# Three attentions of a gated cross-attention stack: reordering one hand-written step and choosing experts for four batches at once

## The chip, the cores and the metric

One NeuronCore of a Trainium2 chip runs the whole program. The metric is the device time of one execution in microseconds (us); a run of the kernel before is quoted as the median of three executions. The engines work side by side, each in the order of its own queue: TensorE (PE, with its weight loads shown as PEld), VectorE (DVE), ScalarE (ACT), GpSimd (POOL), and SyncE (SP), whose queue issues the DMAs. PSUM, into which TensorE writes, has eight banks here, and the kernel uses each bank as one tile.

## The reference, cut to what matters

A batch of 16 sequences of 128 tokens with 256 features passes through four layers. Each layer is a cross-attention and a feed-forward part, each gated by a tanh and added to the residual stream `x`. The change lies in the attentions of layers 0, 1 and 2 (16 heads of 16 features) and in the routing of layer 1's feed-forward part.

```python
x = x + tanh(g_xattn[0]) * xattn0(layernorm(x), ctx)          # 16 heads of 16
x = x + tanh(g_ffn[0])   * experts0(layernorm(x))             # one of 8 experts per token
x = x + tanh(g_xattn[1]) * xattn1(layernorm(x), ctx, rel, mask)
x = x + tanh(g_ffn[1])   * experts1(layernorm(x))             # two of 8 experts, plus a shared one
x = x + tanh(g_xattn[2]) * xattn2(layernorm(x), ctx)
x = x + tanh(g_ffn[2])   * softmoe2(layernorm(x))
...                                                            # layer 3: 16 heads of 64, then a key memory

# routing of layer 1
scores = softmax(xt @ gate_w.T)
_, indices = top_k(scores + gate_bias, 2)
weights = take_along_axis(scores, indices, axis=1)
```

## The kernel before, in words

`xattn16` computes one attention with 16 heads of 16 as a software pipeline over the 16 batches. A loop over a step number `t` calls a list of stages in a fixed order, and each stage works on batch `t - lag`. Inside `tc.manual_schedule` this call order is the order of the instructions on PE, ACT, DVE and POOL, so the list is the schedule. SP's DMAs are issued in their own queue.

In one step the stages do this, in the order before:

1. `bias_load` and `bias_make` (layer 1 only): load mask and relative-time tiles, then turn the mask into an addend: one POOL operation (`mf`, L1399) and three on DVE (L1401 to L1403).
2. `exps` (lag 4): 16 exponentials with accumulated sums on ACT (L525). In layers 0 and 2 they read the score banks in PSUM; in layer 1 the scores have already been moved to SBUF by DVE.
3. `add` and `join`: the gated residual additions on DVE (L236), in `join` of rows fetched from the previous expert stage.
4. `norm.stats` and `after.stats`: mean and variance on DVE, then a reciprocal root on POOL (`ve`, `rs`, L180 and L181), for this attention's norm and for the norm behind it.
5. `choose` (lag 9): the choice of experts from the router's logits, all on DVE. `logits` (lag 8): the router product on PE (`pr`, L657) and its first operations; in layer 1 these are a maximum on DVE (`red`, L944) and an exponential on ACT (`lg`, L947).
6. `norm.apply`, `after.apply` (`xn` or `k`, L212, on DVE, waiting for POOL's root; some also store `xn` by DMA), and `output_bias` (POOL, L483).
7. `turn` (lag 5): 16 transposes of the probabilities on PE into four banks (`pe`, L544), copied to SBUF (`eT`): all four on ACT in layer 1 (L549); two on DVE (L547) and two on ACT in layers 0 and 2.
8. Projections: `keys` or `queries` in turn, every second step each (`pk`/`kT`, `pq`/`qT`), and `value_rows` (`pv` on PE, `v` on DVE, L438).
9. `normalise` (lag 4): POOL multiplies the probabilities by their reciprocal sums (L538).
10. `scores` (lag 3): 8 matrix products into four banks (`sc`, L494), read by DVE at once: four maxima (`mx`, L503) in layers 0 and 2, or 16 fused additions with a minimum (L508) in layer 1.
11. `output` (`po`, L572), `norm.turn` (`pt`), `values` (`av`, L559) and `after.turn` (`pt`), with ACT copies `xqT`, `oT` (L565) and `rT` or `xnT`.

A step with a router takes 15 banks from the eight, a step without one 14. They are handed out in the order in which they come free. In the steady steps of layers 0 and 2 the fourth score bank (`sc3`) is the one that the first ACT copy `eT` of the same step leaves; the bank for `pv` is the one that the first DVE copy `eT` leaves. In layer 1 `sc1` takes the bank of `pv` once DVE has read it, `sc2` the router's bank once ACT has made `lg`, and `sc3` the one that the first `eT` leaves.

After the loop, `Routing.solve` places all tokens in expert order (DVE, with small products on PE), and the expert stage follows on PE.

Of the kernel before, what the change touches and what calls it, by code (L numbers as in the profile page):

```python
# [12 lines left out]
F32 = mybir.dt.float32  # L13
I32 = mybir.dt.int32
BF16 = mybir.dt.bfloat16
AF = mybir.ActivationFunctionType
ALU = mybir.AluOpType
AX = mybir.AxisListType

P = 128  # L20
B, S, D = 16, 128, 256
# [4 lines left out]
SENT = -1.0e30  # L26
FOUND = 1.0e30
# [6 lines left out]
def flamingo_gated(ctx: ExitStack, tc: tile.TileContext, a, out):  # L34
    nc = tc.nc
# [5 lines left out]
    small = ctx.enter_context(tc.tile_pool(name="small", bufs=6))  # L41
# [6 lines left out]
    def broadcast(ap, n):  # L48
        return ap.rearrange("(o n) -> o n", o=1).to_broadcast([P, n])
# [17 lines left out]
    def gate_f(layer):  # L67
        return gates[:, 4 + layer : 5 + layer]
# [9 lines left out]
        out=before, in_=ones, compare_op=ALU.is_gt, fill=0.0, base=0, pattern=[[1, P]], channel_multiplier=-1  # L78
    )
    def counting(n, step, name):  # L80

        i = const.tile([P, n], I32, name=f"{name}i")
        nc.gpsimd.iota(i, pattern=[[step, n]], base=0, channel_multiplier=0)
        f = const.tile([P, n], F32, name=name)
        nc.vector.tensor_copy(f, i)
        return f

    count = counting(P, 1, "count")
# [4 lines left out]
    part = const.tile([P, 1], F32, name="part")  # L93
# [19 lines left out]
    def load_slot(src, cols, name, queue=nc.sync):  # L113
        t = wp.tile([P, WSLOT], F32, tag="w", name=name)
        queue.dma_start(out=t[:, 0:cols], in_=src)
        return t
# [108 lines left out]
    def in_groups(tiles, n, make):  # L225


        def into(b):
            if b % n == 0:
                tiles[b // n] = make()  # L230
            return tiles[b // n][:, :, b % n * S : (b % n + 1) * S]

        return into
# [156 lines left out]
    def xattn16(layer, bias=None, after=None, joining=None):  # L390
# [7 lines left out]
        after, logits, choose = after  # L398
        with ExitStack() as es:
# [186 lines left out]
            if joining is not None:  # L586
# [3 lines left out]

            stages = (
                (1, bias_load),
                (2, bias_make),
                (4, exps),
                (7, add),
                (0, join if joining is not None else None),
                (0, norm.stats),
                (7, after.stats),
                (9, choose),
                (8, logits),  # L600
                (0, norm.apply),
                (7, after.apply),
                (0, output_bias),
                (5, turn),
                (3, value_rows),
                (4, normalise),
                (3, scores),
# [3 lines left out]
                (7, after.turn),  # L611
            )
            with tc.manual_schedule(engines=ENGINES):
                for t in range(-1, B + 9):
                    for lag, stage in stages:
                        if stage == value_rows:
                            if t % 2 and (t + 1) // 2 < B // G:
                                keys((t + 1) // 2)
                            if t % 2 == 0 and 0 < t // 2 <= B // G:
                                queries(t // 2 - 1)  # L620
                        if stage is not None and 0 <= t - lag < B:
                            stage(t - lag)


# [5 lines left out]
    def pick_mask(pool, vals, best, k, mask):  # L630

        top = pool.tile([P, 8], F32, tag="top", name="top")
        nc.vector.memset(top, SENT)
        nc.vector.tensor_copy(top[:, 0:k], best[:, 0:k])
        rep = pool.tile([P, 16], F32, tag="rep", name="rep")
        nc.vector.match_replace(out=rep, in_to_replace=top, in_values=vals, imm_value=FOUND)
        nc.vector.tensor_scalar(mask, rep[:, 0:8], FOUND, None, ALU.is_equal)
# [3 lines left out]
    class Routing:  # L641
# [18 lines left out]
        def choose(self, b, vals):  # L660
            best = self.pool.tile([P, 8], F32, tag="best", name="best", bufs=2)
            nc.vector.max(out=best, in_=vals)
            pick_mask(self.pool, vals, best, 1, self.masks[0][:, b, :])
            if len(self.masks) > 1:
                pick_mask(self.pool, vals, best, 2, self.all[:, b, :])
                nc.vector.tensor_tensor(self.masks[1][:, b, :], self.all[:, b, :], self.masks[0][:, b, :], ALU.subtract)
            nc.vector.tensor_tensor(self.cum[:, b + 1, :], self.cum[:, b, :], self.all[:, b, :], ALU.add)

        def solve(self):
# [254 lines left out]
    def attention_ffn1(joining):  # L924
        with tc.tile_pool(name="r1", bufs=1) as rp:
            wr = rp.tile([P, 2, 8], F32, name="wr1")
            nc.sync.dma_start(out=wr, in_=a["rw1"])
            gb = rp.tile([P, 8], F32, name="gb1")
            nc.sync.dma_start(out=gb, in_=broadcast(a["gb1"], 8))
            routing = Routing(1, rp, 2, NBLK1, wr)  # L930
            vals = [rp.tile([P, 16], F32, tag=f"lg{i}", name=f"lg{i}") for i in range(2)]
            for t in vals:
                nc.gpsimd.memset(t, SENT)
            weights = [const.tile([P, B], F32, tag=f"wt{i}", name=f"wt{i}") for i in range(2)]
            xnT = {}

            into = in_groups(xnT, 4, lambda: xtp.tile([P, 2, GT], F32, tag="xnT", name="xnT"))

            known = {}

            def logits(b):
                pr = routing.logits(b, xnT[b // 4][:, :, b % 4 * S : (b % 4 + 1) * S])
                red = small.tile([P, 1], F32, tag="red1", name="red")
                nc.vector.tensor_reduce(red, pr, AX.X, ALU.max, negate=True)  # L944
                lg = small.tile([P, 8], F32, tag="lg1", name="lg")
                tot = small.tile([P, 1], F32, tag="tot1", name="tot")
                nc.scalar.activation(lg, pr, AF.Exp, bias=red, accum_out=tot)  # L947
                known[b] = lg, tot

            def choose(b):  # L950
                lg, tot = known.pop(b)
                nc.vector.reciprocal(tot, tot)
                nc.vector.scalar_tensor_tensor(vals[b % 2][:, 0:8], lg, tot, gb, ALU.mult, ALU.add)
                nc.vector.tensor_tensor(tot, tot, gate_f(1), ALU.mult)
                routing.choose(b, vals[b % 2])
                for t, m in zip(weights, routing.masks):
                    own = small.tile([P, 8], F32, tag="own1", name="own")
                    nc.vector.scalar_tensor_tensor(own, lg, tot, m[:, b, :], ALU.mult, ALU.mult)
                    nc.vector.tensor_reduce(t[:, b : b + 1], own, AX.X, ALU.add)

            attention1((Norm(into, store=normed[1]), logits, choose), joining)
            ws = load_slot(a["we1"][8], 3072, "ws")
            routing.solve()

            def shared():
                shared_expert(ws, 512, xnT, gate_f(1))

            sorted_experts(routing, a["we1"][0:8], 512, shared)
        return results[1], 2, lambda i, b: weights[i][:, b : b + 1]
# [557 lines left out]
```

## Time and profile before

| what | value |
|---|---|
| median of 3 runs | 2210.04 us (2206.56 to 2211.8) |
| profiled execution, its own time | 2212.79 us |
| its span, first to last instruction | 2211.1 us |
| mean granted TensorE clock | 0.936 of full speed |
| busy: PE, DVE, ACT, POOL | 88%, 58%, 43%, 35% of the span |
| attention of layer 0 | about 24 to 207 us |
| attention of layer 1 | about 436 to 657 us |
| attention of layer 2 | about 990 to 1185 us |

The three attentions fill about 600 us. A step of the loop can be timed by the ACT copy `oT` (L565), of which there is one in each step with values. In layer 0 these copies start at 112.13, 122.51 and 132.89 us, so a step takes 10.38 us. In layer 1 they start at 530.02, 541.14, 552.80 and 566.07 us: steps of 11.12, 11.66 and 13.27 us. In layer 2 they start at 1045.26, 1055.99 and 1068.35 us: 10.73 and 12.36 us.

The lists of stretches, waits, and instructions in order of time are read like this: a bracket behind an instruction gives the idle time of the engine before it and the instruction whose end ended it. PEclk is the share of full speed that TensorE was granted.

### The profile page before, as it was taken

The numbers are of one execution on the slowest core, as the hardware profiler recorded it, in microseconds if no ns is written. First come the engines' busy times: TensorE is split into PE (matmuls) and PEld (weight loads), VectorE is DVE, ScalarE is ACT, GpSimd is POOL, SyncE is SP. The second block draws the span as 40 slices with busy tenths as digits, with TensorE's granted clock in tenths as the row PEclk, the third lists the DMA queues.
The fourth block names the chain that finished last, engine by engine and source line by source line (L and its number), as shares of the span: only waits on it lengthen the run. The fifth ranks groups of instructions, "written<-read, shape, count | busy, mean of one in ns | idle before, by whom it ended". The sixth has DMA issues, their size and how long they took to land.

```text
span 2211.1 us, 31775 instructions
## 1 busy us (share of the span) xinstructions
PE 1948.9 (88%) x10603; PEld 1319.0 (60%) x10603; DVE 1291.9 (58%) x3965; ACT 957.7 (43%) x3103; POOL 769.3 (35%) x921
## 2 busy tenths in 40 slices
PE   5996999888859999978887998949899999988787
PEld 4774566566645666655664444438776777765676
DVE  3776122267773222227766999859926667652775
ACT  5884222288851122228872111134424344434662
POOL 3653333255430145535543222200011222221675
PEclk9998999989879999999998999979999999999788
DMA  2002777511012288873002113543210000000000
GB/s 91 33 23 80 301 293 294 179 37 34 26 30 88 98 311 320 314 261 122 25 18 108 67 76 143 189 168 114 77 39 1 11 11 1 20 2 0 8 13 20
DMA packets 56563, 223.48 MB, mean 101 GB/s; under 512 B 11984, under 2 KB 31952, under 8 KB 44240
## 3 DMA queue, kind: packets, MB, share of 16 engines
q0 software_dynamic: 15312, 134.10, 16.6%
q1 hardware_dynamic: 41088, 87.36, 11.4%
q8 instruction: 84, 1.38, 0.3%
q14 instruction: 79, 0.65, 0.1%
HBM read 190.24 MB, written 31.20 MB: 100 GB/s over the span
## 4 chain that ended last, share of the span: by engine, by line
PE 25%; DVE 19%; POOL 4%; issue 4%; ACT 3%; DMA 1%; POOLq 0%; ACTq 0%; SPq 0%; DVEq 0%
PE pk L266 3%; PE pq L278 2%; PE po L361 2%; PE pv L289 2%; DVE tot L1135 2%; POOL rn L1300 2%; PE po L1155 2%; DVE d L1082 1%; DVE red L1079 1%; DVE tot L1086 1%; PE av L351 1%; DVE cw L1129 1%; PE sc L308 1%; PE pq L1237 1%; DVE cw L1137 1%
## 5 line engine op out<-in xcount | busy, mean ns | idle before, releaser
L803 PE MATMUL pg<-we,xT 128*128 128x512 f32 (+1 forms) x588 | 268.2, 586 | 1.0 <-ACT xT L197 1.0
L538 POOL TENSOR_TENSOR e<-e,sums 128x512 f32<-128x512 f32 x192 | 194.1, 1043 | 144.4 <-DVE sums L533 106.9
L809 DVE TENSOR_TENSOR h<-sg,pg 128x256 f32<-128x256 f32 x147 | 60.3, 411 | 248.0 <-ACT sg L808 201.8
L808 ACT ACTIVATE sg<-pg 128x256 f32<-128x256 f32 x147 | 55.3, 376 | 303.0 <-PE pg L803 295.5
L525 ACT ACTIVATE e<-sc,mx 128x128 f32<-128x128 f32 x512 | 179.7, 413 | 0.0
L803 PEld LDWEIGHTS pg<-we,xT 128*128 128x128 f32 x588 | 106.2, 192 | 89.1 <-issue 79.1
L778 POOL DMA_INDIRECT we<-in_we,rows x62 | 60.0, 967 | 264.3 <-PE pd L834 172.7
L834 PE MATMUL pd<-we,hT 128*128 128x256 f32 (+1 forms) x588 | 141.7, 383 | 1.2 <-ACT hT L823 1.2
L329 POOL TENSOR_TENSOR e<-e,rec 128x512 f32<-128x512 f32 x64 | 65.3, 1041 | 216.7 <-DVE rec L328 140.3
L834 PEld LDWEIGHTS pd<-we,hT 128*128 128x128 f32 (+1 forms) x588 | 109.6, 190 | 44.1 <-issue 25.8
L1155 PE MATMUL po<-yt,cT 128*128 128x256 f32 x512 | 128.2, 396 | 8.5 <-ACT cT L1147 8.4
L1098 PE MATMUL acc<-d,k 128*128 128x512 f32 x256 | 122.4, 620 | 9.7 <-POOL d L1088 9.5
L525 ACT ACTIVATION_READ_ACCUMULATOR e<-sc,mx 128x1 f32 x512 | 129.4, 253 | 0.0
L1088 POOL TENSOR_TENSOR d<-d,tot 128x1024 f32<-128x1024 f32 x32 | 62.8, 1961 | 168.4 <-DVE tot L1087 168.4
L494 PE MATMUL sc<-kT,qT 32*128 32x256 f32 x768 | 98.3, 432 | 25.0 <-DVE v L438 14.0
L1083 ACT ACTIVATE d<-d 128x1024 f32<-128x1024 f32 x32 | 33.8, 1057 | 195.5 <-DVE d L1082 189.2
L1072 PE MATMUL pl<-phi,xnT 128*128 128x512 f32 x256 | 116.5, 599 | 0.0
L544 PE MATMUL pe<-ident,e 128*128 128x128 f32 x768 | 104.1, 289 | 10.4 <-POOL e L538 10.2
L1155 PEld LDWEIGHTS po<-yt,cT 128*128 128x128 f32 x512 | 97.4, 200 | 21.4 <-ACT cT L1147 9.7
L180 POOL TENSOR_SCALAR ve<-mv 128x1 f32<-128x1 f32 (+1 forms) x136 | 26.1, 192 | 234.2 <-DVE mv L187 183.4
L544 PEld LDWEIGHTS pe<-ident,e 128*128 128x128 f32 x768 | 92.0, 152 | 17.2 <-POOL e L538 15.5
L236 DVE SCALAR_TENSOR_TENSOR x<-po,gates,x 128x256 f32<-128x256 f32 x96 | 45.4, 473 | 91.5 <-PE po L361 53.2
(291 smaller groups left out, 4538.4 us busy)
## 6 DMA issues: line engine op xcount, KB each, us to landing
ew<-in_ew SPq DMA_DIRECT2D x8, 2048.0 KB
spill<-lg SPq DMA_DIRECT2D x32, 512.0 KB
cw<-spill SPq DMA_DIRECT2D x8, 2048.0 KB
ctxT<-in_ctxT SPq DMA_DIRECT2D x16, 512.0 KB
got<-results SPq DMA_DIRECT2D x48, 128.0 KB
normed<-xn SPq DMA_DIRECT2D x32, 128.0 KB
aw<-in_aw SPq DMA_DIRECT2D x3, 1280.0 KB
x<-in_x SPq DMA_DIRECT2D x16, 128.0 KB
```

Source lines behind the costliest of these rows:

```text
L266: nc.tensor.matmul(pk, lhsT=wk[:, k, c * P : (c + 1) * P], rhs=ctxT[g][:, k, :], start=(k == 0), stop=(k == 1))
L329: nc.gpsimd.tensor_tensor(e, e, rec.unsqueeze(2).to_broadcast([P, 4, S]), ALU.mult)
L494: nc.tensor.matmul(banks[j][:, c * 256 : (c + 1) * 256].rearrange("p (i k) -> p i k", i=2), lhsT=qT[r, c, tok], rhs=kT[r, c, :, tok], star ...
L525: nc.scalar.activation(e[:, c, :], sc[:, c, :], AF.Exp, bias=mx[:, h : h + 1], scale=sign, accum_out=sums[b][:, h : h + 1],)
L538: nc.gpsimd.tensor_tensor(e, e, r, ALU.mult)
L544: nc.tensor.transpose(pe[:, c * P : (c + 1) * P], e[:, c, :], ident)
L803: nc.tensor.matmul(pg[:, 0 : 2 * m].rearrange("p (g i) -> p g i", g=2), lhsT=tokens[j][:, k, :], rhs=wgu[:, k, :, i0 : i0 + m], start=(k = ...
L834: nc.tensor.matmul(pd[:, 0:D], lhsT=hT[0:m, ic, :], rhs=wd[0:m, ic, :], start=(ic == 0), stop=(ic == nic - 1))
L1072: nc.tensor.matmul(pl, lhsT=xnT[b // 4][:, k, tok], rhs=phi[:, k, n], start=(k == 0), stop=(k == 1))
L1088: nc.gpsimd.tensor_tensor(dv, dv, tot.unsqueeze(2).to_broadcast([P, 32, 32]), ALU.mult)
L1098: nc.tensor.matmul(acc[hf][k][q], lhsT=keep[b][:, k * P : (k + 1) * P], rhs=d[:, q * 512 : (q + 1) * 512], start=(b == 0), stop=(b == B - 1),)
L1155: nc.tensor.matmul(pos[b][:, 0:D], lhsT=cT[:, c, :], rhs=yt[2 * q + c // 2][:, c % 2, :], start=(q == 0 and c == 0), stop=(q == 3 and c == 3),
```

## The change

First, four entries of the stage list move, for all three layers. `turn` goes from behind `output_bias` to a place right behind `choose`, so that its copies stand between the statistics and the norms. `logits` goes behind `bias_make`, and both go behind `output_bias`, ahead of `value_rows`. All other stages keep their order.

Second, in layer 1 `choose` no longer handles one batch per step. It collects four batches and does their work in three parts at three successive steps: scaled probabilities, sums with the bias, four maxima and two copies in the first; eight match-and-replace operations and two mask operations in the second; the second mask, the running counts and the weights in the third; nothing in the fourth. The loop is two steps longer, so that the last group can finish. The gate on the weights is applied once, at the end, to all of them.

Third, the counting line of `Routing.choose` becomes a method `count`, and its branch for two picks, which only layer 1 used, goes away. Layer 0 does the same work as before.

```diff
             stages = (
                 (1, bias_load),
-                (2, bias_make),
                 (4, exps),
...
                 (9, choose),
-                (8, logits),
+                (5, turn),
                 (0, norm.apply),
                 (7, after.apply),
                 (0, output_bias),
-                (5, turn),
+                (2, bias_make),
+                (8, logits),
                 (3, value_rows),
...
-                for t in range(-1, B + 9):
+                for t in range(-1, B + 11):
...
-                        if stage is not None and 0 <= t - lag < B:
+                        if stage is not None and 0 <= t - lag < B + (2 if stage == choose and layer == 1 else 0):
                             stage(t - lag)
...
             def choose(b):
-                lg, tot = known.pop(b)
-                nc.vector.reciprocal(tot, tot)
-                nc.vector.scalar_tensor_tensor(vals[b % 2][:, 0:8], lg, tot, gb, ALU.mult, ALU.add)
-                nc.vector.tensor_tensor(tot, tot, gate_f(1), ALU.mult)
-                routing.choose(b, vals[b % 2])
-                for t, m in zip(weights, routing.masks):
-                    own = small.tile([P, 8], F32, tag="own1", name="own")
-                    nc.vector.scalar_tensor_tensor(own, lg, tot, m[:, b, :], ALU.mult, ALU.mult)
-                    nc.vector.tensor_reduce(t[:, b : b + 1], own, AX.X, ALU.add)
+                part, g = (b + 1) % 4, slice(b // 4 * 4, b // 4 * 4 + 4)
+                if part == 0:
+                    nc.vector.reciprocal(tot[:, g], tot[:, g])
+                    nc.vector.tensor_tensor(lg[:, g, :], lg[:, g, :], wide(tot[:, g]), ALU.mult)
+                    nc.vector.tensor_tensor(vals[:, :, 0:8], lg[:, g, :], gb.unsqueeze(1).to_broadcast([P, 4, 8]), ALU.add)
+                    best = rp.tile([P, 4, 8], F32, tag="best4", name="best4")
+                    for i in range(4):
+                        nc.vector.max(out=best[:, i, :], in_=vals[:, i, :])
+                    for k, t in enumerate(tops):
+                        nc.vector.tensor_copy(t[:, :, 0 : k + 1], best[:, :, 0 : k + 1])
+                elif b >= 4 and part == 1:
+
+                    g = slice(g.start - 4, g.start)
+                    for t, mask in zip(tops, (routing.masks[0], routing.all)):
+                        rep = rp.tile([P, 4, 16], F32, tag="rep4", name="rep4", bufs=2)
+                        for i in range(4):
+                            nc.vector.match_replace(
+                                out=rep[:, i, :], in_to_replace=t[:, i, :], in_values=vals[:, i, :], imm_value=FOUND
+                            )
+                        nc.vector.tensor_scalar(mask[:, g, :], rep[:, :, 0:8], FOUND, None, ALU.is_equal)
+                elif b >= 4 and part == 2:
+                    g = slice(g.start - 4, g.start)
+                    first, both = routing.masks[0][:, g, :], routing.all[:, g, :]
+                    nc.vector.tensor_tensor(routing.masks[1][:, g, :], both, first, ALU.subtract)
+                    for i in range(g.start, g.stop):
+                        routing.count(i)
+                    for t, m in zip(weights, routing.masks):
+                        own = rp.tile([P, 4, 8], F32, tag="own4", name="own4")
+                        nc.vector.tensor_tensor(own, lg[:, g, :], m[:, g, :], ALU.mult)
+                        nc.vector.tensor_reduce(t[:, g], own, AX.X, ALU.add)
+                    if g.stop == B:
+                        for t in weights:
+                            nc.vector.tensor_scalar(t, t, gate_f(1), None, ALU.mult)
```

## The prediction

> **What bounds the kernel now.** I read the page first: PE is busy for 88% of the span, but the three attentions that the change touches are not alike, so I took them stretch by stretch (length, then busy time of PE, PEld, DVE, ACT and POOL with instruction counts, granted clock, DMA share, GB/s). One step of the first attention, two of the second, one of the third:
>
> ```profile
> 112.13:122.51 10.38, 9.86 (x90) 7.59 (x89) 7.86 (x24) 8.39 (x39) 6.35 (x10) 1.00 0.04 14
> ```
> ```profile
> 541.50:553.20 11.70, 9.43 (x88) 7.32 (x88) 10.00 (x68) 10.27 (x45) 6.69 (x11) 1.00 0.06 18
> 553.20:566.50 13.30, 11.01 (x88) 8.12 (x88) 10.80 (x74) 11.36 (x46) 7.59 (x12) 0.87 0.07 18
> ```
> ```profile
> 1045.26:1055.99 10.73, 8.73 (x86) 6.54 (x86) 8.58 (x18) 8.34 (x40) 6.21 (x10) 1.00 0.08 25
> ```
>
> No engine fills its step; each step is a ring through several engines. Next the waits of 440 to 660 us (total, times, longest), then the instructions around one release in order of time:
>
> ```profile
> PEld sc L494 <- DVE v L438: 17.8, 14, 2.3
> ...
> PEld pr L657 <- ACT xnT L197: 11.7, 16, 0.9
> ...
> DVE f L1401 <- POOL mf L1399: 7.7, 13, 1.2
> ```
> ```profile
> 548.51 2.04 ACT L549 COPY eT<-pe 128x512 f32<-128x512 f32 x4
> ...
> 549.25 1.14 PE L494 MATMUL sc<-kT,qT 32*128 32x256 f32 x14 [1.77 <-DVE v L438]
> ...
> 553.35 0.40 ACT L525 ACTIVATE e<-e,mx 128x128 f32<-128x128 f32 x1
> ```
>
> The second attention has two rings of equal length. **DVE's:** its last L508 ends at 541.81, `v` ends at 549.19, `sc` starts at 549.25, L508 again at 550.03, the last one ends at 553.49: 11.7 us. **ACT's:** exponentials from 541.70, `lg` at 548.25, first `eT` done at 549.10, the rest of `sc`, then `po`, `pt`, `av`, `pt`, the copy `xnT`, exponentials at 553.35: 11.65 us. In steps with `kT`, ACT's own work is the bound: 11.1 us without an idle moment (530.4 to 541.5).
>
> In the first attention only ACT's ring is closed: the copies start, `sc` waits for the first, and the tail follows:
>
> ```profile
> 118.23 1.17 ACT L549 COPY eT<-pe 128x512 f32<-128x512 f32 x2
> ...
> 118.97 0.72 PEld L494 LDWEIGHTS sc<-kT,qT 32*128 32x128 f32 x10 [0.18 <-ACT eT L549]
> ...
> 120.03 1.13 PE L572 MATMUL po<-aw,oT 128*128 128x256 f32 x4
> ```
>
> In the third, the chain of waits (start, length, what) runs through DVE and POOL:
>
> ```profile
> 1081.83 0.56 POOL rs L181
> 1082.39 0.03 issue
> 1082.41 0.81 DVE k L212
> 1083.22 0.61 DVE eT L547
> 1083.83 0.04 issue
> 1083.87 1.13 PE pv L434 x4
> 1085.00 1.23 PE sc L494 x14
> ```
>
> The reader is to see that `eT` stands idle behind a norm that waits for POOL, and that PE waits for `eT` to free a bank.
>
> **Part 1: the turn between statistics and norms (third attention).** DVE ends its statistics at 1081.08. POOL's two roots need until 1082.39, in which DVE waits 0.42 and 0.49 us. The two copies (1.28 us) now fill this time; the transposes they read were done by then. `pv` gets its bank at about 1081.1 + 0.64 = 1081.7 instead of 1083.8, and DVE's ring is 2.1 us shorter. What is late next is ACT's ring: from exponentials at 1079.24 to those at 1089.55, 10.31 us. So a step of 10.73 becomes 10.31, not 8.6. By the copies `oT`, steps at 1045.26, 1055.99, 1109.95 and 1120.68, and parts of slow ones at 1068.35 and 1132.16, are above 10.31, by 1.6 us together and some 0.5 for the parts: **2.1 us**. The norms and their DMA stores come 1.3 us later, but their PE readers stand 4 us behind; SP's queue holds nothing that waits for them. POOL's `output_bias` also moves by 1.3 us into 2.7 us of idle time. Cover gone, that would cost 1.3 us a step.
>
> In the first attention the same move does nothing on the ring: DVE waited 1.14 us for `pv` anyway.
>
> **Part 2: the router product behind the turn (first and second).** PE waits 0.46 to 0.52 us in each step for `rT` or `xnT` ahead of `pr`. That wait goes, as transposes fill it. Its sum over 16 steps is 8.2 us in the first attention and 7.4 in the second. It is mostly not a gain: PE reaches `sc` earlier and waits there for ACT. In the first attention a step stays at 10.38; only two steps of the drain, where PE leads, lose 0.5 each: **1 us**. The trace can't show the new hand-out of banks. `pr` no longer takes the first free bank and no longer leaves one for the fourth transposition tile, so each later tile draws another. Ends: `sc` a copy later, +0.2 us a step for 12 steps, +2.4; or `sc3` gets a bank free before the copies, and the ring opens to PE's 9.86, -0.5 for 14 steps, -7. I take 0, nearest to the row of now.
>
> In the second attention ACT no longer waits for `red` before its copies (0.29 us ahead of `lg` at 548.25) and makes `lg` (0.26) after them. But `lg` then frees the router's bank last, so I count `sc3` on the second copy (+0.48): exponentials 6.2, two copies 1.06, tail 3.8 (from 549.25 to 553.35 are 4.1, less 0.3 for `sc` already done), together **11.1**.
>
> **Part 3: `bias_make` behind `output_bias`.** DVE's wait for `mf` (0.75 us, POOL being in `normalise` until 542.15) goes from the head of the step. It returns smaller or equal behind the norms: `mf` now follows `output_bias`, which follows `xn`, so `f` starts about 1.3 us after `xn` ends, of which the second `xn` covers 0.4. Behind `f` on DVE are `red` and `v`, and PE waits for `v`. The mask load that follows `mf` moves along; it is used a step later.
>
> **Part 4: choice for four.** Before, a batch costs 20 DVE records from 545.16 to 548.06: 2.90 us. The three parts, by the spacing of the same rows: (1) reciprocal 0.16, two 128x32 operations 0.25 each, four maxima 0.15, two copies 0.2: 1.7; (2) eight match-and-replace with value load 0.25, two masks 0.2: 2.4; (3) mask 0.15, four dependent counts 0.17, four for the weights 0.22: 1.7. That is 5.8 for four, or 1.45 a batch. No row shows 128x32 with a broadcast; 0.17 (128x8) to 0.29 (128x128) bounds it, ±0.2 us per group.
>
> DVE from the last L508 to the end of `v`, worked as above, with the roots ready 3.4 us in: 5.8 (empty step), 6.1, 6.6 and 7.1 against 7.37: its ring goes to 10.1-11.3, mean 10.7. ACT's 11.1 is next. So steps with `qT` go from 11.65 to 11.1, four of them: **2.2 us**. Steps with `kT` stay. Later steps (603 to 635 us, 10.43, ACT's ring) lie between -0.26 and +0.3: 0.
>
> The drain: the last choice now takes 5.8 us, but spread behind three steps that no longer carry 2.90 each. Counting from 641.3 (2.4 and 1.7 in the first two, none in the third, then 1.7, 2.4 and up to the counts 0.9) the counts are ready at 656.1, as now (656.29, `pn` starts): 0.
>
> **The clock.** In the second attention the steps ending at 492.23, 505.61, 518.90, 566.07, 578.77 and 592.38 take 12.7 to 13.6 us, together 79.5 against 67.8 at the 11.3 of the others: 11.7 us lost, as `po` takes 2.08 us (562.40) instead of 1.13 (550.32). They begin behind PE gaps of 0.2 to 1.8 us at `sc`. The Trainium skill, "TensorE: Matmul & The Clock Gate", section "Why this matters for your kernels", puts the limit at idle gaps of about 3 us. By that rule no gap here, before or after, costs anything: 0. By the row they do cost. I take the row. PE's idle time in a `qT` step falls from 2.2 us (0.46 at `pr`, 1.77 at `sc`) to 11.1 - 9.43 = 1.7, but in one gap. The bounds are all 11.7 gained, or the same again lost; the first attention with 0.5 idle holds 1.00, the third with 2.0 mostly holds it. I take a third: **4 us**.
>
> The same page, section "Part 4: PE-mode transpose", says that transposes don't count as PE work for this gate. It would speak against a turn put straight behind `pt`'s transposes: 2.4 us of them in a row. The row says otherwise: the first attention has 0.44 + 1.94 us of transposes with only 1 us between and stays at 1.00. By the rule I would add 2 us to a third of 30 steps, +20; by the row 0.
>
> **Sum.** 2.1 + 1 + 2.2 + 4 = 9.3, and 0.9 for the one step of the second attention in which DVE's `red` itself waits for `pr`: 10.2 us. The profiled execution took 2212.8 (span 2211.1 and 1.7 around it), so 2202.6; the median of the runs is 2.8 below it: **2199.8 us**. The stages behind (PE in order behind the placing of tokens) take the whole shift.
>
> **Rivals.**
> - *The banks open ACT's ring.* First attention -7, third: `sc` behind the exponentials alone, 10.31 to 9.85 (ACT's own work with `kT`), 11 steps, -5; with the 10.2: 2187.8. For it: `eT` on DVE frees banks earlier. Against: the copies on ACT keep their place. 0.17.
> - *The clock falls where it held (slower).* Joined gaps at `sc`: about 1 us in the first attention, 1.5 in the third, where a wait at `pv` and one at `sc` were apart. If these drop at half the second's rate (6 of 13 steps), 10 of some 27 steps cost 2.0 more: +20, less the 10.2 and with the 4 us of the clock not gained: +13.8, 2223.8. It decides from five such steps on. For it: a gap of 1.28 us preceded the slow step at 485.34. Against: the third attention, 1.1 to 1.5, mostly holds. 0.22.
> - *Off the ring altogether.* ACT keeps all three, clock as before: -2, 2208. For it: ACT's ring is within 0.1 us of DVE's in the second attention. 0.16.
>
> **How the numbers follow.** Forecast 0.45, own range 2192 to 2206. No change can be told from a measurement within 0.2%, 4.4 us. Faster: 0.17 + nearly all of 0.45: 0.59; same: 0.19; slower: 0.22. The range takes in the opened ring and half of the clock's loss: 2185 to 2219.
>
> **What would show it.** In the third attention, no chain through `rs`, `k`, `eT`, `pv`, and steps near 10.3. In the second, DVE idle over 1 us a step, `sc` waiting for `eT` and not for `v`, `mf` still waited for, steps of 11.1. In the first, `pr` without a wait and 10.38 as before. Steps of 9.9 there show opened banks; clocks below 0.9 there show the slower rival. I am wrong if the second attention's steps stay at 11.65 or PE's clock there is no better than 0.87.

## The result, and the profile after

The change makes the kernel slower: 2228.87 us median of five runs (2219.49 to 2231.65) against 2211.8 for the kernel before (2206.56 to 2212.72), a ratio of 1.0073 with a 95% interval of 1.0047 to 1.0099. A second measurement (change_again below) gave 2225.03 against 2213.38, 1.0048 [1.0031, 1.0066]. The profiled execution is the quickest of the five, 2219.49 us (span 2217.8), so its trace shows 6.7 us of a loss of 12 to 17.

First the stretches of the profile after, one step each, with the columns of the prediction's list (length, busy time of PE, PEld, DVE, ACT, POOL with instructions, granted clock, DMA share, GB/s): a steady step of attention 0, then its three steps that have `pv` but neither `kT` nor `qT`; three steps of attention 1; one of attention 2.

```profile
112.08:122.47 10.39, 10.11 (x90) 7.72 (x90) 7.30 (x24) 8.39 (x40) 6.35 (x10) 1.00 0.05 14
143.24:156.07 12.83, 11.83 (x82) 8.18 (x82) 8.61 (x32) 7.65 (x37) 7.29 (x12) 0.73 0.04 12
166.23:179.13 12.90, 11.42 (x79) 7.91 (x79) 8.23 (x30) 7.28 (x37) 6.01 (x9) 0.74 0.03 11
179.13:192.13 13.00, 11.52 (x79) 7.79 (x79) 6.93 (x21) 7.31 (x37) 4.78 (x7) 0.76 0.17 52
534.60:545.94 11.34, 10.25 (x90) 7.89 (x89) 6.61 (x40) 11.04 (x46) 6.29 (x10) 1.00 0.11 33
545.94:558.88 12.94, 11.88 (x90) 8.85 (x90) 10.21 (x67) 10.07 (x43) 6.89 (x11) 0.87 0.06 17
608.85:622.50 13.65, 10.85 (x79) 7.65 (x79) 8.64 (x66) 9.07 (x40) 5.24 (x8) 0.75 0.04 12
1064.53:1074.85 10.32, 9.49 (x86) 7.19 (x86) 7.54 (x18) 9.43 (x41) 6.34 (x10) 1.00 0.09 27
```

The last steps of attention 0 before, in the same columns:

```profile
143.27:153.17 9.90, 8.45 (x82) 6.07 (x81) 7.76 (x24) 7.65 (x37) 5.87 (x10) 1.00 0.05 16
163.34:173.02 9.68, 8.16 (x80) 5.78 (x79) 6.58 (x21) 7.28 (x36) 4.29 (x6) 1.00 0.05 14
173.02:182.71 9.69, 8.17 (x80) 5.79 (x79) 6.67 (x21) 7.28 (x37) 4.79 (x7) 1.00 0.25 69
```

Steady steps do what was forecast: 10.39 and 10.32. But three steps of attention 0 grow from between 9.7 and 9.9 us to some 13, with the same work on PE, PE busy 3.3 us longer, and the clock down from 1.00 to about 0.75. They add 9.5 us, and attention 0 ends 8.9 us later (`pn`, the first product of the placing of tokens, starts at 214.95 instead of 206.03). The clock of attention 1 from its first `oT` to its last is 0.88, against 0.89 before, and the attention ends with two steps of 13.65 where before they took 10.43.

The waits of attention 1, 440 to 665 us, in the profile after (total, times, longest):

```profile
PEld sc L494 <- ACT eT L549: 18.7, 21, 3.2
...
PEld sc L494 <- DVE v L438: 11.7, 14, 2.7
...
DVE f L1431 <- POOL mf L1429: 10.7, 14, 1.2
```

`pr` is no longer among those that wait long; `sc` now waits for `eT` more than for `v`; DVE's wait for `mf` did not shrink, it grew from 7.7 to 10.7 us.

The chain of waits through one step of attention 2 (start, length, what):

```profile
1069.12 1.68 ACT e L525 x9
1070.80 0.04 issue
1070.84 1.60 PE sc L494 x12
1072.44 1.06 PE po L572 x4
1073.50 0.22 PE pt L196 x2
1073.72 1.05 PE av L559 x32
...
1074.85 0.31 ACT oT L565
```

POOL's roots and the norms are gone from it. What remains is ACT's ring: the exponentials, then `sc`, `po`, `pt` and `av` on PE, a copy, and exponentials again.

### The profile page after: what moved, and what is told of

It is laid out like the page before. It is cut to its first block, busy times and chain, and to the rows that moved or that the text cites. A ratio compares the mean times of both kernels' runs of the same rounds, so it can differ in the third digit from the quotient of the medians.

```text
span 2217.8 us, 31603 instructions
## 1 busy us (share of the span) xinstructions
PE 1964.9 (89%) x10603; PEld 1329.5 (60%) x10603; DVE 1259.6 (57%) x3791; ACT 957.2 (43%) x3103; POOL 770.3 (35%) x922
## 4 chain that ended last, share of the span: by engine, by line
PE 27%; DVE 15%; ACT 5%; issue 3%; POOL 3%; DMA 1%; POOLq 0%; ACTq 0%; SPq 0%; DVEq 0%
ACT e L525 3%; PE pk L266 2%; PE pq L278 2%; PE po L361 2%; PE pv L289 2%; DVE tot L1165 2%; POOL rn L1330 2%; PE po L1185 2%; PE acc L1128 2%; PE pl L1102 1%; PE av L351 1%; DVE cw L1159 1%; PE sc L308 1%; PE pq L1267 1%; DVE cw L1167 1%
## 5 line engine op out<-in xcount | busy, mean ns | idle before, releaser
L525 ACT ACTIVATE e<-sc,mx 128x128 f32<-128x128 f32 x512 | 179.7, 412 | 0.0
L494 PE MATMUL sc<-kT,qT 32*128 32x256 f32 x768 | 119.5, 443 | 36.2 <-ACT e L525 15.1
L1185 PE MATMUL po<-yt,cT 128*128 128x256 f32 x512 | 125.8, 391 | 11.4 <-ACT cT L1177 11.3
L494 PEld LDWEIGHTS sc<-kT,qT 32*128 32x128 f32 x768 | 65.4, 196 | 84.2 <-ACT e L525 33.2
L544 PE MATMUL pe<-ident,e 128*128 128x128 f32 x768 | 101.9, 287 | 10.7 <-POOL e L538 10.6
L1185 PEld LDWEIGHTS po<-yt,cT 128*128 128x128 f32 x512 | 95.5, 196 | 24.0 <-ACT cT L1177 12.8
```

What stands on the lines that cost most here:

```text
L494: nc.tensor.matmul(banks[j][:, c * 256 : (c + 1) * 256].rearrange("p (i k) -> p i k", i=2), lhsT=qT[r, c, tok], rhs=kT[r, c, :, tok], star ...
L525: nc.scalar.activation(e[:, c, :], sc[:, c, :], AF.Exp, bias=mx[:, h : h + 1], scale=sign, accum_out=sums[b][:, h : h + 1],)
L544: nc.tensor.transpose(pe[:, c * P : (c + 1) * P], e[:, c, :], ident)
L1185: nc.tensor.matmul(pos[b][:, 0:D], lhsT=cT[:, c, :], rhs=yt[2 * q + c // 2][:, c % 2, :], start=(q == 0 and c == 0), stop=(q == 3 and c == 3),
```

## Experiments

Each kernel was timed beside the kernel before on the same chip; ratios are to that. Rows with the same value in the third column were timed together; the groups ran on different chips, so a comparison between two groups is rougher than one inside a group.

| kernel | median us | before, beside it | ratio [95%] |
|---|---|---|---|
| choice_alone | 2210.58 | 2213.98 | 0.9982 [0.9971, 0.9994] |
| order_alone | 2227.04 | 2213.98 | 1.0054 [1.0034, 1.0073] |
| old_in_first | 2217.5 | 2213.98 | 1.002 [1.0009, 1.0031] |
| new_in_third | 2209.58 | 2213.98 | 0.9976 [0.9963, 0.999] |
| fill_full | 2216.4 | 2212.9 | 1.0016 [1.0004, 1.0028] |
| fill_turned | 2218.6 | 2212.9 | 1.0019 [1.0007, 1.003] |
| fill_corner | 2225.4 | 2212.9 | 1.0046 [1.0027, 1.0065] |
| router_ahead | 2206.48 | 2212.9 | 0.9973 [0.996, 0.9986] |
| change_again | 2225.03 | 2213.38 | 1.0048 [1.0031, 1.0066] |
| fill_two | 2210.74 | 2213.38 | 0.9991 [0.9977, 1.0005] |
| router_filled | 2204.77 | 2213.38 | 0.9955 [0.9938, 0.9972] |
| fill_in_wait | 2214.34 | 2214.72 | 0.9997 [0.9984, 1.001] |
| change_output_ahead | 2186.87 | 2214.72 | 0.9861 [0.9839, 0.9883] |
| output_ahead | 2172.84 | 2214.72 | 0.9799 [0.9776, 0.9823] |

### Which part costs, and in which attention

Four kernels take the change apart. choice_alone has the choice for four with the list of before; order_alone the new list with the choice of before; the other two use both lists (OLD and NEW stand for the two lists of the diff).

```diff
 # choice_alone: the change with
-            stages = NEW
+            stages = OLD
 # order_alone: the kernel before with
-            stages = OLD
+            stages = NEW
 # old_in_first: the change with
+            if layer in (0,):
+                stages = OLD
 # new_in_third: the change with
+            if layer in (0, 1):
+                stages = OLD
```

> The choice for four, with the order of before in all three attentions. Theory A (the order costs, through the granted clock; the choice gains): attentions 0 and 2 step as before (10.38 and 10.7 us, PE clock 0.98 and 0.91); in attention 1 DVE ends its step earlier and the time falls by 2 to 6 us, to 2206 to 2210. Theory B (the choice costs: 2 us of it in one step make attention 1 uneven and its end late): 5 to 8 us slower than before, 2217 to 2220.

> The new order of stages in all three attentions, with the choice per batch of before. Theory A: attention 0 loses 9 to 10 us in its steps without keys, at a PE clock of 0.7 to 0.76 there, attention 2 gains 5, attention 1 loses 3 to 10 more than with the choice for four: 2220 to 2232. Theory B: attention 1 is no slower than before, so 2211.8 + 9.4 - 5.1 = 2216.

> The change, but with the order of before in attention 0. Theory A (attention 0 carries most of the loss): oT steps there of 10.38, 9.9 and 9.7 us at a clock of 1.00 again, and 9 us less than the change: about 2219, and less if the runs of the change that were slower than its profiled one lost their time there too. If attention 1 carries the loss of the slower runs: no less than 2219, to 2222.

> The order of before in attentions 0 and 1, the new order in attention 2, and the choice for four. Theory A: 5.1 us gained in attention 2 and 2 to 6 by the choice: 2200 to 2205, faster than both kernels. Theory B: 5 gained in attention 2, 5 to 8 lost by the choice: 2212 to 2215.

The choice gains 3.4 us alone, the order loses 13.1 alone: theory A in both. By differences of medians inside this group, the order costs 2217.5 - 2209.58 = 7.9 us in attention 1 and gains 1.0 in attention 2 (new_in_third against choice_alone, which the intervals do not separate from nothing). In attention 0 it costs about 8, by two groups: change_again lies 11.7 above its before, old_in_first 3.5 above. Theory A had put most of the loss into attention 0; it is half there and half in attention 1. old_in_first came out 1.5 us under the 2219 expected, new_in_third above its 2200 to 2205.

The profiles show why single traces mislead here. With PE's order of before and no added work (before, choice_alone, old_in_first, new_in_third and router_ahead below), 4 of the 15 steps without `kT` or `qT` in attention 0 took over 11 us, though the code of this attention is the same in the first four. With the new order (the change twice, order_alone) it was 9 of 9, each above 12.7 us. In attention 1, the time from the first `oT` to the last was 175.4, 177.9, 179.7 and 175.3 us with the new order (change, change_again, order_alone, old_in_first), and 171.4, 167.1 and 168.2 us with PE's order of before and the choice for four (choice_alone, new_in_third, router_ahead). The one trace of the kernel before has 174.0, with the choice per batch.

### Is it the clock, and what counts as work for it?

Three kernels add products to the change, between `pv` and `sc`, in just those three steps of attention 0. fill_full adds 0.83 us of PE's time to each, and fill_corner 0.84 us on a sixteenth of the array. fill_turned adds only 0.49 us: in the records a transpose of this size is one pass of about 0.27 us, a product two.

```diff
 # in value_rows, behind the products of pv
+                for n in range(3 if layer == 0 and b in (12, 14, 15) else 0):
 # fill_full
+                    nc.tensor.matmul(pv[:, 256:384], lhsT=ident, rhs=ident, start=True, stop=True)
 # fill_turned
+                    nc.tensor.transpose(pv[:, 256:384], ident, ident)
 # fill_corner
+                    nc.tensor.matmul(pv[0:32, 256:384], lhsT=ident[0:32, 0:32], rhs=ident[0:32, :], start=True, stop=True)
```

> The change, and in attention 0's three steps without kT or qT (batches 12, 14, 15 of value_rows) three extra products of the whole array (128x128 into a free part of the bank pv, 0.6 us together) between pv and sc, where PE later waits 0.8 us for ACT. Added work, nothing left out. Theory A (the clock is granted by how much of the array worked in a stretch of 3.41 us; the steps fall because pv and sc stand there without the transposes): the three steps go from 12.8 to 13.0 back to 9.9 and 9.7 us, the clock in them to 1.00, the whole 9 us less than the change. Theory B (the length of the waits decides): the same. Theory D (the steps are long for another reason than the clock, such as banks): 0.6 us more in each.

> The same with three extra transposes of the same size in place of the products. By the rule that transposes do not count as PE work the three steps stay at 12.8 to 13.0 us. Theory A with transposes counted in full, and theory B: 9.9 and 9.7 us, 9 us less than the change.

> The same with three extra products of the same length that use 32 rows and 32 columns of the array, a sixteenth of it. Theory A: hardly any help, the three steps stay at 12.8 to 13.0 us. Theory B (only PE's idle time counts): 9.9 and 9.7 us, as with the others.

fill_full: the three steps take 10.38, 10.15 and 10.15 us at a clock of 1.00 (9.9 and 9.7 were expected; the added products themselves are on the path there), and the whole falls by 0.3 to 0.6% against the change. fill_corner, timed beside it: 13.07, 12.89 and 13.06 us, as without, and a median 9.0 us above fill_full's (2225.4 against 2216.4). Adding work made the kernel faster, and the same PE time on a sixteenth of the array did not, so the clock is the cause in attention 0. fill_turned: 10.38, 11.29 and 12.74 us in its profile, one step kept and two not; its median of 2218.6 lies nearer to fill_full's than to fill_corner's. Transposes do help, and the reading "they stay at 12.8 to 13.0" falls.

The clock in the trace is either whole or half, and changes on a grid of 3.413 us: the recorded stretches last 3.413, 6.827, 10.240 us and so on. The Trainium skill, "TensorE: Matmul & The Clock Gate", section "What's actually happening", says the same: a window of 3413 ns that runs freely and does not start anew with the kernel. So PE's work has to be cut along that grid. Three such stretches of the change, around the beginning of the first long step:

```profile
141.63:145.04 3.41, 3.41 (x54) 2.92 (x52) 3.24 (x14) 2.17 (x10) 2.90 (x6) 1.00 0.26 96
145.04:148.46 3.42, 2.81 (x13) 1.74 (x12) 2.54 (x8) 3.42 (x21) 1.42 (x3) 1.00 0.12 41
148.46:151.87 3.41, 3.02 (x14) 1.73 (x13) 0.77 (x2) 2.06 (x9) 1.88 (x2) 0.50 0.01 5
```

two of the kernel before,

```profile
148.51:151.92 3.41, 2.71 (x18) 1.66 (x17) 1.79 (x4) 2.04 (x9) 1.91 (x2) 1.00 0.01 2
151.92:155.33 3.41, 2.89 (x49) 2.41 (x48) 3.17 (x15) 2.53 (x12) 2.87 (x5) 1.00 0.01 2
```

two of fill_corner,

```profile
146.41:149.82 3.41, 3.35 (x18) 2.21 (x18) 2.17 (x6) 3.41 (x22) 0.99 (x2) 1.00 0.11 38
149.82:153.24 3.42, 2.77 (x13) 1.99 (x14) 1.28 (x3) 1.56 (x6) 2.40 (x3) 0.50 0.01 2
```

and two of fill_full:

```profile
144.53:147.95 3.42, 3.25 (x19) 2.58 (x18) 2.62 (x8) 3.42 (x21) 1.41 (x3) 1.00 0.13 42
147.95:151.36 3.41, 2.71 (x17) 1.68 (x17) 1.30 (x3) 2.04 (x9) 1.90 (x2) 1.00 0.01 4
```

In the kernel before PE is busy for 2.71 us of a stretch and keeps its clock. In fill_corner it is busy for 3.35 us of 3.41, idle for 0.06, and loses it in the next stretch. Idle time is not the measure. What PE did in the change, in order of time (start, length, what; 128*128 or 32*128 is the part of the array that is used, 128x8 or 32x256 the tile; a count is of passes, two for a product and one for a transpose):

```profile
143.05 0.44 PE L196 MATMUL pt<-ident,xn 128*128 128x128 f32 x2
143.32 1.91 PE L544 MATMUL pe<-ident,e 128*128 128x128 f32 x16
145.42 0.61 PE L657 MATMUL pr<-wr,rT 128*128 128x8 f32 x4 [0.18 <-ACT e L525]
146.03 1.13 PE L434 MATMUL pv<-aw,ctxT 128*128 128x256 f32 x4
147.09 0.69 PE L494 MATMUL sc<-kT,qT 32*128 32x256 f32 x2
148.21 1.01 PE L494 MATMUL sc<-kT,qT 32*128 32x256 f32 x2 [0.43 <-ACT e L525]
149.61 2.54 PE L494 MATMUL sc<-kT,qT 32*128 32x256 f32 x12 [0.39 <-ACT e L525]
152.08 2.07 PE L572 MATMUL po<-aw,oT 128*128 128x256 f32 x4
```

and the same step in the kernel before:

```profile
144.03 0.61 PE L657 MATMUL pr<-wr,rT 128*128 128x8 f32 x4 [0.52 <-ACT rT L197]
144.50 1.94 PE L544 MATMUL pe<-ident,e 128*128 128x128 f32 x16
146.28 1.03 PE L434 MATMUL pv<-aw,ctxT 128*128 128x256 f32 x4
147.40 1.53 PE L494 MATMUL sc<-kT,qT 32*128 32x256 f32 x6
149.63 1.13 PE L494 MATMUL sc<-kT,qT 32*128 32x256 f32 x10 [0.70 <-ACT e L525]
150.69 1.13 PE L572 MATMUL po<-aw,oT 128*128 128x256 f32 x4
```

The reader is to see what stands between the last full transpose and `po`, the next full product. Before, they are 4.25 us apart (146.44 to 150.69). With the new order `pr` stands between them too: in fill_full, at a clock of 1.00, they are 5.9 us apart (144.72 to 150.62). A stretch of 3.41 us can then fall between them and hold little but `pr` with its 8 columns, `pv`, a few products `sc` and two waits.

How much is little can be counted. The passes of `pv`, with 256 columns, start 0.216 us apart at full clock, so give each pass 0.216 us times its columns over 256, times its share of the array (rows and columns used, of 128 each), once, in the middle of its record, however long that is. Passes of `sc` on different strips of 32 rows can start 0.007 us apart and overlap, up to four together; by busy time they are counted too high, or, cut to a quarter, too low. The stretch from 145.04 in the change then holds 0.86 us of `pv`, 0.12 of `sc`, 0.11 of transposes and 0.03 of `pr`: 1.12. The one from 148.51 in the kernel before, which keeps the clock, holds 0.61 of `sc`, 0.86 of `po` and 0.18 of a transpose: 1.65. In fill_corner the stretch with 3.35 us of busy time comes to 1.15; in fill_full the two come to 1.78 and 1.28, and the clock holds. In fill_turned's second and third step a stretch of 1.22 and one of 0.65 lose it.

The same count was made for all eight profiles without added work (before, the change twice, the four above, router_ahead), between the first and the last `oT` of the three attentions: 926 stretches at full clock, 113 of them followed by half clock. All 109 with less than 1.24 us were followed by half clock, and none of the 806 with more than 1.32 us; of the 11 between, 4. The eight other profiles, which played no part in setting these two figures, give the same: all 92 below 1.24 and none of 815 above 1.32 are followed by half clock, of 16 between 6. A single bound of 1.28 misplaces 2 of the 926. By plain busy time the best bound misplaces 50, with `sc` counted as a full product 61, and with transposes as nothing 104, hardly fewer than saying "never" (113). So in these kernels the clock is granted by the work done on the array in a stretch, transposes in full, and narrow products by their share.

### Putting PE's order back

```diff
                 (9, choose),
+                (8, logits),
                 (5, turn),
                 (0, norm.apply),
                 (7, after.apply),
                 (0, output_bias),
                 (2, bias_make),
-                (8, logits),
                 (3, value_rows),
```

On PE this is exactly the order of before; the copies `eT` still stand ahead of the norms, `bias_make` still behind. With the product, the operations on DVE and ACT that belong to `logits` (`red` and `lg` in attention 1) go back too.

> The change, with the router product right ahead of the turn again, so that PE's order is that of before, while the copies eT stay ahead of the norms on DVE and ACT. Theory A: attention 0 back at 10.38, 9.9 and 9.7 us with the clock of before, attention 1 no worse than with the choice alone, attention 2 as in the change: 2203 to 2209 us. If the place of the copies is what costs (ACT and DVE, banks): about the time of the change, 2224 to 2230.

2206.48, inside theory A's range, and 0.7 to 1.0% under the change by the ratios. In its profile attention 2 steps at 10.31, attention 1 at 11.12 six times in a row, and one step of attention 0's end is long (12.17). So the place of the stage `logits` carries the loss, and the place of the copies on DVE and ACT none that can be seen. That it is the product on PE and not `red`, `lg` or the hand-out of banks is shown for attention 0 by the fillers; for attention 1 this edit alone doesn't separate them.

### How much of attention 1 is the clock?

```diff
 # fill_two: fill_full, and in attention 1
+                for n in range((0, 3, 0)[layer] if b not in (12, 14, 15) else (3, 6, 0)[layer]):
 # router_filled: router_ahead with
+                for n in range((3, 6, 3)[layer] if b in (12, 14, 15) else 0):
 # fill_in_wait: fill_full, and in scores, four (eight) products ahead of the third bank's first
+                extra = (8 if b in (12, 14, 15) else 4) if layer == 1 else 0
+                        for n in range(extra if (c, j) == (0, 2) else 0):
+                            nc.tensor.matmul(banks[0][:, 256:384], lhsT=ident, rhs=ident, start=True, stop=True)
```

> The change itself, once more, so that the kernels with extra products are set against it on the same chip: 0.6 to 0.8% above before. Its profile should show the three steps of 12.8 to 13.0 us in attention 0 again, and in attention 1 ten or more steps above 12 us, though not the same ones.

> The change with extra products of the whole array between pv and sc in attentions 0 and 1: three in attention 0's steps without kT or qT, three in each step of attention 1 and six in its last three. Added work, nothing left out. Theory A (the loss of attention 1 is the clock too, by the share of the array in a stretch): attention 1 steps at 11.1 to 11.5 us with a clock of 0.95 or more between its first and last oT, and the whole is at or below before, 2200 to 2212 us. Rival (attention 1 loses by its waits for v and eT, which the clock only follows): steps of 12.8 and more stay, 0.6 us are added, 2216 to 2225.

> The router product right ahead of the turn, with three extra products in the steps of batches 12, 14 and 15 in attentions 0 and 2, and six in those of attention 1. Theory A: the steps of 12 to 13.4 us there (one in attention 0, three in 1, two in 2 in the last profile) go to 9.7 to 11, 8 to 12 us less: 2194 to 2199. If the clock is not what makes them long: 2207.

> The change, with the three extra products in attention 0 as in fill_full, and in attention 1 four extra products of the whole array (0.9 us; eight in the steps of batches 12, 14, 15) inside sc, ahead of the third bank, where PE waits 0.5 to 1.1 us for eT. Added work, nothing left out. Theory A (attention 1 loses by the clock, and the stretch that decides is the one with sc and its wait): attention 1 steps at 11.1 to 11.6 us, clock 0.95 or more from its first oT to its last, 8 to 12 us less than fill_two or fill_full: 2200 to 2206. Rival (it loses by the waits): steps of 12.8 to 13.5 remain, 2211 to 2218.

change_again shows the three steps of 12.7 to 13.0 us again; in attention 1 it has eight steps above 12 us, not ten.

fill_two hits its time, 2210.74, for another reason than it gave: attention 1 still has seven steps above 12 us, and a clock of 0.90 from its first `oT` to its last. Many of the added products fell into the stretch of the projections, which was full, and left `sc` and its wait as they were: the stretch from 520.55 us holds 3.24 us of work, the next one 0.86, all of it `sc`, and behind it the clock falls. fill_in_wait puts them there: three steps are above 12 us and the others of full length take 10.6 to 11.5, the clock is 0.96 (0.88 in the change), and the time from the first `oT` to the last is 166.1 us against 175.4 in the change. So in that profile the clock accounts for the loss between these two points. Its median, however, missed: 2214, level with before and not separated from fill_two's or fill_full's ratio. The trace shows where most of the gain went: the time from the attention's first `pk` to its first `oT` is 48.8 us against 42.5 in the change, with the added products in it and a clock of 0.76 against 0.84, so that the attention up to `pn` takes 227.2 us, against 230.1 in the change and 223.9 in router_ahead. How much of attention 1's 8 us is the clock is therefore not measured by a median. It isn't all of it: at a clock of 1.00 its full steps take 11.3 to 11.5 us with the new order and 11.12 in router_ahead, and what makes this difference was not isolated.

router_filled comes to 2204.77, above its forecast of 2194 to 2199; by its interval it isn't told apart from router_ahead. In its profile the long steps at the end of attentions 0 and 1 went (9.90, 9.68, 9.69; 10.64, 11.78, 10.66), those of attention 2 stayed (12.37, 12.05).

### A version that beats both

The chain of attention 2 after has `po` between `sc` and the copies that ACT's next exponentials stand behind. `po` needs nothing of this step. It can go ahead of `sc`, where PE waits.

```diff
                 (4, normalise),
+                (6, output),
                 (3, scores),
-                (6, output),
```

> The change, with po ahead of sc on PE in all three attentions, so that PE's wait inside sc falls behind po's 1.1 us of work and the tail behind sc is shorter by as much. If the ring through ACT and the tail is what paces the steps: 10.4 and 10.3 us go to 9.9 in attentions 0 and 2, 11.1 to about 10.6 in 1, 10 to 17 us less. Theory A on the clock: less waiting in all, but sc stands further from a product of the whole array: the steps without keys stay slow. Together 2205 to 2220. If the banks that po takes earlier hold up sc: no gain, 2225 or more.

> The router product right ahead of the turn, and po ahead of sc. By the shorter tail 5 to 15 us less than the router product alone: 2192 to 2202. If the steps are paced by something else, or banks hold up sc: 2206 or more.

Together with router_ahead's order this takes 42 us off the kernel before: 2172.84, 0.9799 [0.9776, 0.9823], below the forecast of 2192. By the ratios `po` ahead of `sc` brings 1.7% of it. Steps are 9.85 us in attention 0, 9.44 in 2 and 10.74 to 10.97 in most of 1. The chain of waits in attention 2 of output_ahead:

```profile
1054.80 1.90 PE pk L419 x8
1056.70 0.96 PE pv L434 x4
1057.66 0.86 PE po L572 x4
1058.52 2.00 PE sc L494 x16
1060.53 0.37 PE pt L196 x2
1060.89 1.01 PE av L559 x32
1061.90 0.37 PE pt L196 x2
1062.28 0.90 PE pe L544 x8
```

It is PE from end to end: no wait at `sc`, no engine between. Most of the gain is the shorter ring: at a clock of 1.00 in both, steps of attention 2 take 9.44 us instead of router_ahead's 10.31. The clock of attention 2 rises as well, from 0.94 to 0.96 between first and last `oT`. The same edit on the change gives 2186.87, also below its forecast of 2205; in attention 0 four of the steps that take 9.85 us in output_ahead take 10.38 there and the fifth 12.07, so the router product behind the turn costs in this version too (14.0 us between the two medians). Why it holds 10.38 was not followed up.

## Why the prediction was wrong

The forecast was 2199.8, faster; in direction and size the slower rival ("the clock falls where it held", 2223.8) is what happened, at 2225 to 2229. The rest of the forecast's mechanics mostly stands.

- **Bound before, and Part 1 (attention 2).** Right. Seven steps in a row take 10.32 or 10.33, forecast 10.31, and the chain left POOL and DVE for ACT's ring, as named. By medians the gain is 1.0 us, which the intervals do not separate from nothing; forecast 2.1.
- **Part 2, attention 0.** The steady step (10.38) is right, and so "I take 0" for the banks. The drain is wrong: not 1 us gained but 9 lost.
- **Part 2 and 4, attention 1.** The choice: with the order of before, steps with `qT` take 11.12 us, forecast 11.1 from 11.65, and the kernel 3.4 us less, forecast 2.2. With the change's order steps at a clock of 1.00 take 11.3 to 11.5. The 0.9 us for `red` waiting for `pr` was not won: it waits 5.2 us in five places after, against 0.9 in one before; what that costs was not isolated. `mf` is waited for 3 us longer in sum, not equal or less; router_ahead has `bias_make` in the same place and steps at 11.12, so that costs nothing that shows. The drain, forecast at 0, gained 1.7 us in the profile (13.9 us before, 12.2 after, from the last `oT` to `pn`).
- **The clock, the step that failed.** "I take a third: 4 us" gained in attention 1, and "by the row 0" for attention 0. Measured: the order costs about 8 us in each, 13.1 alone in all. In attention 0 this is the clock; in attention 1, by the profiles, the clock is a large part, not the whole. The term was built on PE's idle time in a step (2.2 against 1.7 us), and idle time doesn't decide: a stretch with 0.06 us idle lost the clock, one with 0.70 kept it. What decides is the work in a stretch of 3.41 us, and that it fell in the drain of attention 0 (the two stretches above: 1.65 before, 1.12 after) was not looked for. The prediction's own sign of being wrong, a clock in attention 1 no better than 0.87, came true: 0.87 from 445 to 665 us. That attention 2 holds its clock with 2.0 us idle was taken as a sign that joined waits are harmless; but attention 2 has no router product, so there the change moves nothing on PE at all.
- **The two rules weighed.** The skill's rule of about 3 us of idle time, quoted in the prediction, would have given 0; the runs are against it: the clock halved behind waits of 0.18 and 0.43 us. The rule that transposes don't count was rightly refused (fill_turned, and 104 misplaced stretches against 2), but the reason given, that attention 0 had as many transposes and held, looked at how many stood in a row and not at which neighbours they leave without them. Its +20 is nearer to the +13 than the 0 taken, by a mechanism that the fillers contradict: that is luck.
- **The slower rival.** It named the waits at `sc`, and "joined gaps" as its cause; it was to decide from five slow steps on. That its 2223.8 lies so near is partly luck: it put ten slow steps of 2.0 us each into the first and the third attention. The first had three, at +3.2 us on the mean, the rest of the loss came in the second, and the third lost nothing. The cause is finer: the wait at `sc` matters because little work stands around it, and the transposes that used to stand nearer were moved away.

## What to carry to other kernels

Moving an instruction on PE changes what each 3.4 us of PE's time is made of; list the neighbours of its thinnest products (few rows, few columns, waits) before and after, by columns times share of the array and not by busy time. Where PE waits inside such a group, fill the wait with full products that are due anyway: `po` ahead of `sc` did that and shortened the ring at the same time, for 1.7%. Products that are not due cost PE time of their own, as the beginning of attention 1 in fill_in_wait shows. And compare the order on the engine itself first: an attention without the moved instruction says nothing on what moving it does.

## What the runs showed of the hardware

- Extra full products made the kernel faster: three in each of three steps took 0.83 us of PE time per step, and the median was 9.0 us lower than with products of the same length on a sixteenth of the array (2216.4 against 2225.4).
- The granted clock fell behind a stretch in which PE was busy for 3.35 of 3.41 us: 8 columns, a sixteenth of the array or a quarter of the rows in much of it, so that its work comes to 1.15 us of the whole array.
- In 1849 stretches of the three attentions, from sixteen profiles, the clock halved behind every one with less than 1.24 us of such work and behind none with more than 1.32 us.
- The grid of 3.413 us runs free of the kernel, and the same code of attention 0 had none, one or two long steps in different executions; medians over many runs (22 for choice_alone, 2204.14 to 2220.37) separate what one trace can't.
